# A four-layer convolution kernel: six-row sums in PSUM, border copies and a gate product on GpSimd, taps loaded a call ahead, box products behind the copies

## The chip, the cores and the metric

The kernel runs on one core of one Trainium2 chip. A core has five engines with in-order instruction queues of their own: TensorE (PE in the profile; PEld is its weight loads) for matrix products and transposes, VectorE (DVE) and ScalarE (ACT) for elementwise work, GpSimd (POOL), and SyncE (SP), which here only issues transfers. They work on two on-chip memories, SBUF and the smaller PSUM, which is cut into eight banks of 128 x 512 float32 values and into which TensorE writes; GpSimd has no part in PSUM anywhere in this kernel. Sixteen DMA engines move data to and from device memory; transfers are issued from the queues of SP, ACT and POOL. Engines wait for each other through semaphores. The metric is the device time of one execution in microseconds, and lower is better.

## The reference, cut to what matters

The input is x of shape (4, 384, 64, 64) in float32: four images, 384 channels. Four layers follow one another, and each adds its result to x: attention, a convolution with a Fourier filter in 8x8 patches, a token-mixing layer, and a 7x7 depthwise convolution whose filter depends on the image. The change concerns the end of the third layer and all of the fourth:

```python
# end of layer 2: h2 is a normalised hidden result, gate one number per image
ch = tok + h2
x = x + gate * ch + (1.0 - gate) * xn
# layer 3, on xn = group norm of x
x_w = gelu(x_avg @ w_avg.T + b_avg + x_max @ w_max.T + b_max)
xr = (x_w[:, :, None] * w_mix[None]).reshape(b, c, 7, 7)
Gx = sqrt(sum(xr * xr, axis=(2, 3)))
Nx = Gx / (mean over channels of Gx + 1e-6)
kern = gamma * (xr * Nx) + beta          # 7x7, one per image and channel
out = depthwise 7x7 convolution of xn with kern, zero padding 3
x = x + out
```

Since xr is one number per image and channel times a fixed 7x7 filter w_mix, the last convolution falls into two parts: a number times the convolution with w_mix, and beta times a 7x7 box sum. The kernel computes them apart and adds both to x.

## The kernel before, in words

Channels are in three tiles of 128 (NJ = 3, index j), each with four images (b) of 4096 pixels. Phases A, B and EF do the first three layers. Phase G (`phase_g`, L1686) is the last stage, and all that the change touches lies in it.

The code is written as Python generators that emit pieces of work in turn. A scheduler then orders the emitted instructions on each engine by their dependencies and its own estimates, so the order on an engine is close to, but not the same as, the order of the text. Tiles come from pools with a tag and a number of buffers: a tile's next use of a buffer waits for the last reader of its earlier use.

*The gate.* `x2_of(j, b)` (L1886) finishes x for one tile and image in four quarters of 1024 pixels: it loads a quarter of h2 (L1899, tag w7, three buffers), ScalarE multiplies and shifts it into a PSUM bank (L1903, two of 512), VectorE adds it to x (L1906), ScalarE sums squares (L1908) and VectorE takes the maximum (L1909). The finished x goes to device memory through GpSimd's queue (L1911). For tile 0, `to_strips` (L1914) at once makes the strips of the convolution from it: ScalarE scales (L1925), TensorE transposes (L1935), ScalarE and VectorE copy into the large SBUF tile z (L1942, L1940). For tiles 1 and 2 `half_strips` (L1848) does that later from device memory.

*The conv.* `conv7(j, c0)` (L1945) convolves eight channels with w_mix. Sixteen calls make one tile, 48 calls all three. A call loads its taps (L1950, 256 KB, through SP's queue, two buffers), makes four Toeplitz matrices from them and a band (L1959: two of three by VectorE with the band in PSUM, one of three by GpSimd with the band in SBUF), and multiplies them on TensorE with z (L1972) into a PSUM tile of 1024 columns (two banks, two buffers). For tiles 0 and 1 ScalarE copies the result out (L1981) and it goes to device memory (L1982); for tile 2 VectorE adds it to x from the box part (L1984), and the sum is output (L1985).

*The boxes.* `boxes(j, b)` (L1987) makes the 7x7 box sum of one tile and image in four parts of 16 rows. GpSimd adds pairs of rows (L2021) and neighbouring pairs (L2023); VectorE makes six-row sums in place (L2024) and adds to each the seventh row, which gives seven-row sums (L2029, L2030, L2034, with L2027 and L2038 at the image's border). Rows of the part before that a part needs are copied by ScalarE (L2003, L2016), and ScalarE fills border rows (L2008). TensorE transposes 4 x 128 columns at a time (L2044), ScalarE copies them to SBUF (L2046, tile ht), TensorE multiplies with a band matrix (L2050), which sums along the row, and VectorE scales and adds to x (L2052). For tiles 0 and 1 VectorE then adds the conv result, read back from device memory (L2062), and x is output (L2066); for tile 2 it goes to device memory (L2068) for `conv7` to add to.

*The order.* `phase_g` first runs the gate and the strips of tile 0, then for each tile the sixteen conv calls. After each call it takes pieces of other generators: with tile 0 the gate of tiles 1 and 2, with tiles 1 and 2 the boxes (first those of tile 2, then tile 0, then tile 1), and half strips of the tile that comes next. The boxes give up control three times a part, at these lines of the loop:

```python
            yield                       # L2039, after the seven-row sums
            for q in range(2):
                ...
                if q == 0:
                    yield               # L2053, after the first half
            ...
            yield                       # L2069, after the part
```

PSUM in this phase: three banks with tag m (`pm`), one for the band, four for the conv (two tiles of two banks).

## Time and profile before

| what | value |
|---|---|
| median of 3 runs | 4842.55 us (4839.95 to 4853.89) |
| the profiled execution's own time | 4841.52 us |
| its span in the profile | 4839.6 us, 49747 instructions |
| busy in the span: PE, DVE, ACT, POOL | 91%, 60%, 41%, 16% |
| phase G in the span | about 4070 to 4839.6 us |
| mean granted TensorE clock | 0.95 |

The busy shares are those of the whole span, in which the earlier phases weigh most: there TensorE alone is full. Phase G is read by stretches of its own. In it the first tile's gate ends at about 4163 us, the other gates at about 4362 us, and the rest is conv and boxes. A line of the profile names the line of the kernel, the engine, the operation, what it writes and reads and in what shape; a mean that is far above the median says that some of these instructions stood waiting after they had begun. In the chain of waits, "A <- B: total, times, longest" says how long A's engine sat idle until B was done.

### The profile page before, as it was taken

The page shows a single profiled execution, that of the slowest core. Times are in us where ns is not written, and L with a number is a line of the kernel's source. Part 1 is how long each engine was busy: PE and PEld are TensorE (multiplying, and loading weights), DVE is VectorE, ACT ScalarE, POOL GpSimd, SP SyncE. Part 2 cuts the span into 40 slices and gives each one's busy share as a digit, 9 for nine tenths or more (in the row PEclk, how much of TensorE's full clock was granted, in tenths as well). Part 3 has the DMA queues.
Part 4 walks back from the last instruction along what each step waited for, and adds up shares of the span by engine and source line. Part 5 has one row for each costly group of instructions (what it writes and reads, how often), then busy time and mean ns, then how long its engine had stood idle before and what let it go on. Part 6 is the DMA issues. An engine that isn't in the chain of part 4 may idle for free.

```text
span 4839.6 us, 49747 instructions
## 1 busy us (share of the span) xinstructions
PE 4399.5 (91%) x18445; PEld 2453.7 (51%) x18445; DVE 2892.0 (60%) x4647; ACT 1996.9 (41%) x2976; POOL 757.7 (16%) x643
## 2 busy tenths in 40 slices
PE   6999999999999999989987898699999997778888
PEld 2233444344443444435477787344444443678888
DVE  7766556645656455556867777555521113767898
ACT  4444444444444444336345566211133334763321
POOL 1000000000000000000044554000000001235544
PEclk9999999999999999989988999899999998788999
DMA  4312212111211111113168898776664444995776
GB/s 145 102 42 66 72 53 75 64 56 42 70 61 63 40 59 59 53 63 120 65 197 282 278 308 299 273 259 251 238 236 153 156 156 152 325 346 183 231 256 232
DMA packets 289663, 747.65 MB, mean 154 GB/s; under 512 B 22555, under 2 KB 123014, under 8 KB 277382
## 3 DMA queue, kind: packets, MB, share of 16 engines
q1 hardware_dynamic: 226744, 454.62, 29.4%
q0 software_dynamic: 36480, 167.01, 9.2%
q10 hardware_dynamic: 26190, 122.76, 6.4%
q8 instruction: 149, 2.44, 0.2%
q14 instruction: 100, 0.82, 0.1%
HBM read 442.04 MB, written 302.25 MB: 154 GB/s over the span
## 4 chain that ended last, share of the span: by engine, by line
PE 32%; DVE 7%; DMA 6%; ACT 3%; issue 2%; POOL 1%; SPq 0%; ACTq 0%; DVEq 0%; POOLq 0%
PE h_m L1658 10%; PE h_s L1604 10%; PE conv_m L1370 6%; PE conv_m L1972 2%; DMA c_d<-d 2%; DMA wmix<-in_mix_t 1%; DMA g_h<-h 1%; DVE toep L1959 1%; PE box_m L2050 1%; DVE in_x L2052 1%; DMA ax<-x 1%; DVE in_x L2062 1%; DMA unit_x<-x 1%; DVE box L2034 0%; ACT g_h L1908 0%
## 5 line engine op out<-in xcount | busy, mean ns | idle before, releaser
L819 ACT ACTIVATE probs<-sc_s 128x1024 f32<-128x1024 f32 x512 | 496.5, 1019 | 695.0 <-PE av L929 594.8
L929 PE MATMUL av<-probs,vt 128*128 128x512 f32 x1536 | 717.7, 604 | 0.0
L1128 DVE SCALAR_TENSOR_TENSOR acc<-band,vecs,acc 128x512 f32<-128x512 f32 x708 | 496.0, 745 | 44.9 <-POOL band L1089 39.6
L1658 PE MATMUL h_m<-f_h,cm_w_t 128*128 128x512 f32 x1152 | 497.3, 595 | 7.4 <-ACT f_h L1646 7.4
L1370 PE MATMUL conv_m<-toep,z 128*128 128x192 f32 (+1 forms) x2304 | 444.2, 354 | 9.5 <-DVE z L1299 9.4
L929 PEld LDWEIGHTS av<-probs,vt 128*128 128x128 f32 x1536 | 277.6, 192 | 339.6 <-issue 335.9
L1972 PE MATMUL conv_m<-toep,z 128*128 128x128 f32 x3072 | 395.5, 287 | 36.5 <-POOL toep L1959 15.8
L1370 PEld LDWEIGHTS conv_m<-toep,z 128*128 128x128 f32 x2304 | 408.5, 197 | 31.6 <-DVE z L1299 10.1
L1972 PEld LDWEIGHTS conv_m<-toep,z 128*128 128x128 f32 x3072 | 381.1, 203 | 38.4 <-POOL toep L1959 16.2
L1604 PE MATMUL h_s<-e_tok,cm_w_t 128*128 128x512 f32 x768 | 362.9, 595 | 4.2 <-DVE e_tok L1589 4.2
L1658 PEld LDWEIGHTS h_m<-f_h,cm_w_t 128*128 128x128 f32 x1152 | 220.4, 191 | 284.4 <-issue 273.3
L1666 DVE BATCH_NORM_STATS2 h_st<-f_h 128x6 f32<-128x512 f32 x96 | 66.5, 694 | 429.8 <-ACT f_h L1665 429.8
L811 PE MATMUL sc_s<-q,k 32*128 32x512 f32 x2048 | 307.1, 643 | 15.1 <-ACT probs L819 14.9
L1351 POOL TENSOR_TENSOR toep<-w,band 128x1280 f32<-128x1280 f32 x94 | 272.6, 2900 | 237.5 <-PE conv_m L1370 234.3
L1051 PE MATMUL t_m<-w_in_t,xb 128*128 128x384 f32 x768 | 282.0, 503 | 3.4 <-DVE coef L1068 3.2
L965 PE MATMUL proj_m<-xm,w_proj_t 128*128 128x512 f32 x576 | 270.3, 609 | 6.4 <-DVE xm L904 4.9
L1611 ACT COPY e_h<-h_s 128x1024 f32<-128x1024 f32 x96 | 97.2, 1012 | 400.2 <-PE h_s L1604 400.2
L1613 DVE BATCH_NORM_STATS2 h_st<-e_h 128x6 f32<-128x512 f32 x192 | 123.4, 685 | 204.9 <-ACT e_h L1611 204.7
L1604 PEld LDWEIGHTS h_s<-e_tok,cm_w_t 128*128 128x128 f32 x768 | 146.9, 191 | 187.9 <-issue 183.1
L1051 PEld LDWEIGHTS t_m<-w_in_t,xb 128*128 128x128 f32 x768 | 144.4, 194 | 141.6 <-issue 62.5
L972 DVE SCALAR_TENSOR_TENSOR x_res<-proj_m,bn_c,x_res 128x512 f32<-128x512 f32 x96 | 71.7, 747 | 240.2 <-PE proj_m L965 240.2
L1604 PE MATMUL h_s<-z,cm_w_t 128*128 128x512 f32 x384 | 196.7, 594 | 0.0
(423 smaller groups left out, 6396.3 us busy)
## 6 DMA issues: line engine op xcount, KB each, us to landing
d<-d_o ACTq DMA_DIRECT2D x48, 1024.0 KB
c_d<-d SPq DMA_DIRECT2D x48, 1024.0 KB
hid<-e_h ACTq DMA_DIRECT2D x16, 3072.0 KB
f_h<-hid SPq DMA_DIRECT2D x16, 3072.0 KB
x_in<-in_x SPq DMA_DIRECT2D x96, 256.0 KB
x_res<-in_x SPq DMA_DIRECT2D x32, 768.0 KB
xa<-x_res POOLq DMA_DIRECT2D x32, 768.0 KB, 3.9
xa_out<-xa SPq DMA_DIRECT2D x32, 768.0 KB
```

The costliest lines, as they stand in the source:

```text
L811: nc.tensor.matmul(s[:, g], lhsT=k4[32 * g : 32 * g + 32, c], rhs=q[i][32 * g : 32 * g + 32], start=True, stop=True,)
L819: nc.scalar.activation(p[:, h * 1024 : (h + 1) * 1024], s[:, 2 * h : 2 * h + 2].rearrange("p a b -> p (a b)"), AF.Exp, scale=0.25,)
L929: nc.tensor.matmul(av[0], lhsT=vt[:, 4 * c + v, :], rhs=p[:, v * 512 : (v + 1) * 512], start=c == 0 and v == 0, stop=c == 7 and v == 3,)
L965: nc.tensor.matmul(m, lhsT=self.w_proj[:, j, o * P : (o + 1) * P], rhs=xm[:, j], start=j == 0, stop=j == NJ - 1,)
L1051: nc.tensor.matmul(m[:, 0:C], lhsT=xb[:, j], rhs=self.w_in[:, j, :], start=j == 0, stop=j == NJ - 1,)
L1128: nc.vector.scalar_tensor_tensor(out, src(j, k), w, done, ALU.mult, ALU.add)
L1351: eng.tensor_tensor(t, self.w53[:, at : at + 160].rearrange("p (m n) -> p m n", n=8).unsqueeze(2).to_broadcast([P, 20, 8, 8]), band.rearra ...
L1370: nc.tensor.matmul(m[:, c * 256 + to : c * 256 + to + 64 * (k1 - k0)], lhsT=self.z_[:, at : at + P], rhs=t[:, 10 * c + k0 : 10 * c + k1].r ...
L1604: nc.tensor.matmul(s[:, v, :], lhsT=w1[:, j, o * P : (o + 1) * P], rhs=t[j][:, v * 512 : (v + 1) * 512], start=j == 0, stop=j == NJ - 1,)
L1613: nc.vector.bn_stats(st[:, o, 8 * b + 2 * i + v, :], h[:, o, v * 512 : (v + 1) * 512])
L1658: nc.tensor.matmul(m, lhsT=w2[:, o, j * P : (j + 1) * P], rhs=h[:, o, v * 512 : (v + 1) * 512], start=o == 0, stop=o == 5,)
L1972: nc.tensor.matmul(m[:, ch * P : (ch + 1) * P], lhsT=self.z_[:, at : at + P], rhs=t[:, 8 * c + 2 * i : 8 * c + 2 * i + 2].rearrange("p m a ...
```

## The change

The change has six parts, all in phase G.

- *Taps.* `load_mix` loads the taps of a call and keeps the tile in `mix_ahead`. It is called once before the loop, and each `conv7` takes that tile and calls it for the next call. The load is issued through GpSimd's queue instead of SP's.
- *conv7 as a generator.* `conv7` gives up control after each of its four matrices and at its end, and the loop takes the pieces of other generators there, five a call as before. Its PSUM tile is one bank of 512 columns, three buffers, and is copied out (or added) after every second matrix, in two halves instead of one.
- *Gate product of tile 0.* For j = 0, GpSimd multiplies and shifts h2 in place in SBUF, and VectorE adds 1024 columns at once from SBUF. Every second quarter takes its buffer from the pool with the tag rest, so that six are in use instead of three. For tiles 1 and 2 nothing changes.
- *Border rows.* The two row copies in `boxes` move from ScalarE to GpSimd. The fill reads a constant instead of x.
- *Six-row sums.* VectorE writes the six-row sum to a PSUM bank of its own (tag t) instead of back to SBUF, and the lines after it read it there. PSUM: three banks m, one band, three conv, one t.
- *Box products.* The product with the band matrix and the scaled addition move into `box_sums`, which is called after a yield that follows the ht copy, for both halves; the yield at the end of a part is gone, so there are still three.

```diff
@@ -1751,13 +1751,14 @@
             x2 = others(*(self.x2_of(j, b) for j in (1, 2) for b in range(B)))
             boxes = others(*(self.boxes(j, b) for j, b in ((2, 0), (2, 1), (2, 2), (2, 3), (0, 0), (0, 1), (0, 2), (0, 3))))
             boxes1 = others(*(self.boxes(1, b) for b in range(B)))
+            self.load_mix(0)
             for j in range(NJ):
                 for half in range(2):
                     strips = self.half_strips(j + half, 1 - half) if 0 < j + half < NJ else iter(())
                     for n in range(8):
-                        self.conv7(j, 64 * half + 8 * n)
-                        next(strips, None)
-                        for k in range(5):
+                        for k, _ in enumerate(self.conv7(j, 64 * half + 8 * n)):
+                            if k == 0:
+                                next(strips, None)
                             if j == 0 and (k < 2 or k == 2 and n % 2):
                                 next(x2, None)
                             if j == 1 or j == 2 and (k or n % 2):
@@ -1895,15 +1896,20 @@
         for q in range(4):
             sl = slice(q * 1024, (q + 1) * 1024)
 
-            h = self.gw_p.tile([P, 1024], F32, tag="w7", name="g_h2", bufs=3)
+            pool, tag = (self.gt_p, "rest") if j == 0 and q % 2 else (self.gw_p, "w7")
+            h = pool.tile([P, 1024], F32, tag=tag, name="g_h2", bufs=3)
             nc.sync.dma_start(h, self.h2[b][:, j, sl])
-            for v in range(2):
-                m = self.pm("x2_m")
-                part = slice(q * 1024 + v * 512, q * 1024 + v * 512 + 512)
-                nc.scalar.activation(
-                    m, h[:, v * 512 : v * 512 + 512], AF.Identity, bias=at(self.g0), scale=at(self.gh)
-                )
-                nc.vector.tensor_add(x[:, part], x[:, part], m)
+            if j == 0:
+                nc.gpsimd.tensor_scalar(h, h, at(self.gh), at(self.g0), ALU.mult, ALU.add)
+                nc.vector.tensor_add(x[:, sl], x[:, sl], h)
+            else:
+                for v in range(2):
+                    m = self.pm("x2_m")
+                    part = slice(q * 1024 + v * 512, q * 1024 + v * 512 + 512)
+                    nc.scalar.activation(
+                        m, h[:, v * 512 : v * 512 + 512], AF.Identity, bias=at(self.g0), scale=at(self.gh)
+                    )
+                    nc.vector.tensor_add(x[:, part], x[:, part], m)
 
             nc.scalar.activation(h, x[:, sl], AF.Square, bias=at(self.neg2), accum_out=self.x2_var[:, j, b, q : q + 1])
             nc.vector.tensor_reduce(self.x2_max[:, j, b, q : q + 1], x[:, sl], AX.X, ALU.max)
@@ -1942,17 +1948,26 @@
                     nc.scalar.copy(zv, mv.rearrange("p k c -> p c k"))
             yield
 
+    def load_mix(self, n):
+        if n < 16 * NJ:
+            c0 = n % 16 * 8
+            self.mix_ahead = self.gt_p.tile([P, 8 * 64], F32, tag="wmix", name="wmix")
+            src = self.ins["mix_t"][n // 16][:, c0 : c0 + 8]
+            self.nc.gpsimd.dma_start(self.mix_ahead, src.rearrange("p c t n -> p (c t n)"))
+
     def conv7(self, j, c0):
 
 
         nc = self.nc
-        wmix = self.gt_p.tile([P, 8 * 64], F32, tag="wmix", name="wmix")
-        nc.sync.dma_start(wmix, self.ins["mix_t"][j][:, c0 : c0 + 8].rearrange("p c t n -> p (c t n)"))
+        wmix = self.mix_ahead
+        self.load_mix(16 * j + c0 // 8 + 1)
         o = self.gt_p.tile([P, 8, P], F32, tag="rest", name="rest_o", bufs=3)
         if j == NJ - 1:
             nc.sync.dma_start(o, self.rest[c0 : c0 + 8].rearrange("c y b n -> (y b) c n"))
-        m = self.psum.tile([P, 1024], F32, tag="c", name="conv_m", bufs=2)
+        of = o.rearrange("p c n -> p (c n)")
         for pair in range(4):
+            if pair % 2 == 0:
+                m = self.psum.tile([P, 512], F32, tag="c", name="conv_m", bufs=3)
             t = self.gt_p.tile([P, 16, 8, 8], F32, tag="toep", name="toep", bufs=4)
             on_pool = (c0 // 2 + pair) % 3 == 2
             eng, band = (nc.gpsimd, self.band7) if on_pool else (nc.vector, self.band7_p)
@@ -1970,19 +1985,24 @@
                 for i in range(4):
                     at = (c0 + ch) * 136 + 4 * i
                     nc.tensor.matmul(
-                        m[:, ch * P : (ch + 1) * P],
+                        m[:, ch % 4 * P : (ch % 4 + 1) * P],
                         lhsT=self.z_[:, at : at + P],
                         rhs=t[:, 8 * c + 2 * i : 8 * c + 2 * i + 2].rearrange("p m a n -> p (m a n)"),
                         start=i == 0,
                         stop=i == 3,
                     )
-        of = o.rearrange("p c n -> p (c n)")
+            if pair % 2:
+                part = of[:, pair * 256 - 256 : pair * 256 + 256]
+                if j < NJ - 1:
+                    nc.scalar.copy(part, m)
+                else:
+                    nc.vector.tensor_add(part, part, m)
+            yield
         if j < NJ - 1:
-            nc.scalar.copy(of, m)
             nc.scalar.dma_start(self.raw[j][:, c0 : c0 + 8], o)
-            return
-        nc.vector.tensor_add(of, of, m)
-        nc.sync.dma_start(self.out[j][:, c0 : c0 + 8], o)
+        else:
+            nc.sync.dma_start(self.out[j][:, c0 : c0 + 8], o)
+        yield
 
     def boxes(self, j, b):
 
@@ -1991,7 +2011,6 @@
         nc = self.nc
         x = self.load_x2(j, b)
         off = lambda k: self.off[:, j, b, k - 6 : k - 5]
-        scale = self.b_s[:, j, b : b + 1]
         pairs_of = lambda t, r, n: t[:, r * W : (r + 2 * n) * W].rearrange("p (k r w) -> p k r w", r=2, w=W)
         above, last = None, None
         for part in range(4):
@@ -2000,20 +2019,20 @@
             if part < 3:
 
                 above = self.sm([P, 2, W], "edge")
-                nc.scalar.copy(above, pairs_of(x, r0 + 12, 2)[:, :, 1])
+                nc.gpsimd.tensor_copy(above, pairs_of(x, r0 + 12, 2)[:, :, 1])
 
             s = self.gw_p.tile([P, 10, W], F32, tag="w", name="box_2")
             t = self.gw_p.tile([P, 8, W], F32, tag="w6", name="box_6")
             h = self.gw_p.tile([P, 16 * W], F32, tag="w7", name="box_7", bufs=3)
             fill = lambda i: nc.scalar.activation(
-                s[:, i], x[:, r0 * W : (r0 + 1) * W], AF.Identity, bias=self.off[:, j, b, 2:3], scale=0.0
+                s[:, i], self.ident[:, 0:W], AF.Identity, bias=self.off[:, j, b, 2:3], scale=0.0
             )
             lo, hi = 2, 10
             if part == 0:
                 fill(0)
                 lo = 1
             else:
-                nc.scalar.copy(s[:, 0:2], last[:, 8:10])
+                nc.gpsimd.tensor_copy(s[:, 0:2], last[:, 8:10])
             if part == 3:
                 fill(9)
                 hi = 9
@@ -2021,7 +2040,9 @@
             nc.gpsimd.tensor_add(s[:, lo:hi], xv[:, :, 0], xv[:, :, 1])
             last = s
             nc.gpsimd.tensor_add(t, s[:, 0:8], s[:, 1:9])
-            nc.vector.tensor_add(t, t, s[:, 2:10])
+            six = self.psum.tile([P, 512], F32, tag="t", name="box_t", bufs=1).rearrange("p (k w) -> p k w", w=W)
+            nc.vector.tensor_add(six, t, s[:, 2:10])
+            t = six
             hv = pairs_of(h, 0, 8)
             if part == 0:
                 nc.vector.tensor_scalar(hv[:, 0:2, 0], t[:, 0:2], off(6), None, ALU.add)
@@ -2044,14 +2065,11 @@
                     nc.tensor.transpose(m[:, k * P : (k + 1) * P], h[:, at : at + P], self.ident)
                 ht = self.gt_p.tile([P, 512], F32, tag="ht", name="ht")
                 nc.scalar.copy(ht, m)
-                m = self.pm("box_m")
-                for k in range(4):
-                    sl = slice(k * P, (k + 1) * P)
-                    nc.tensor.matmul(m[:, sl], lhsT=ht[:, sl], rhs=self.cols7, start=True, stop=True)
-                xq = x[:, (2 * part + q) * 512 : (2 * part + q + 1) * 512]
-                nc.vector.scalar_tensor_tensor(xq, m, scale, xq, ALU.mult, ALU.add)
                 if q == 0:
                     yield
+                    self.box_sums(j, b, x, 2 * part, ht)
+            yield
+            self.box_sums(j, b, x, 2 * part + 1, ht)
             if j < NJ - 1:
                 d = self.gt_p.tile([P, 1024], F32, tag="rest", name="in_raw", bufs=3)
                 nc.sync.dma_start(
@@ -2066,7 +2084,16 @@
                     nc.gpsimd.dma_start(self.out[j].rearrange("(b m) c n -> b (m c n)", b=B)[b].rearrange("(c n) -> c n", c=P), x)
                 else:
                     nc.gpsimd.dma_start(self.rest[:, :, b], x.rearrange("p (y n) -> p y n", n=P))
-            yield
+
+    def box_sums(self, j, b, x, n, ht):
+
+        nc = self.nc
+        m = self.pm("box_m")
+        for k in range(4):
+            sl = slice(k * P, (k + 1) * P)
+            nc.tensor.matmul(m[:, sl], lhsT=ht[:, sl], rhs=self.cols7, start=True, stop=True)
+        xq = x[:, n * 512 : (n + 1) * 512]
+        nc.vector.scalar_tensor_tensor(xq, m, self.b_s[:, j, b : b + 1], xq, ALU.mult, ALU.add)
 
 
 @with_exitstack
```

## The prediction

> **What bounds the kernel now.** Everything that the change touches runs after 4070 us, so I first cut the last stage into four stretches (busy time by engine, then granted clock, DMA share, GB/s): the gate of the first channel tile, the conv of that tile with the other gates, and two halves of conv and boxes.
>
> ```profile
> core 0: us, PE busy (x) PEld busy (x) DVE busy (x) ACT busy (x) POOL busy (x), PEclk, DMA share, GB/s
> 4077.00:4163.00 86.00, 34.35 (x132) 22.85 (x132) 58.08 (x76) 80.64 (x105) 9.14 (x19) 0.52 0.87 310
> 4163.00:4362.00 199.00, 156.25 (x1228) 153.72 (x1228) 136.28 (x157) 118.59 (x171) 64.24 (x39) 0.88 0.95 340
> 4362.00:4610.00 248.00, 214.70 (x1735) 208.14 (x1736) 207.55 (x249) 89.76 (x162) 134.94 (x99) 0.94 0.68 206
> 4610.00:4840.00 230.00, 193.60 (x1573) 188.48 (x1571) 208.53 (x210) 45.60 (x94) 105.13 (x64) 0.93 0.73 241
> ```
>
> Stretch 1 is ScalarE's (80.6 of 86), with DMA close behind. Stretch 2 is the DMA engines': share 0.95, in most of it 0.97 to 0.99. Stretches 3 and 4 have two near-bounds at once, TensorE and VectorE; in stretch 4 VectorE leads (it has nothing to do after 4828).
>
> Second, VectorE's own lines (min/median/max ns), to see whether 208 us is work or waiting:
>
> ```profile
> L2024 DVE TENSOR_TENSOR box<-box,box x48: 660/690/2882, 4367.2 to 4803.2; 128x512 f32<-128x512 f32 x48
> L2029 DVE SCALAR_TENSOR_TENSOR box<-edge,off,box x36: 317/344/4112, 4374.9 to 4804.9; 128x128 f32<-128x128 f32 x36
> L2052 DVE SCALAR_TENSOR_TENSOR in_x<-box_m,b_s,in_x x96: 727/740/752, 4377.4 to 4827.9; 128x512 f32<-128x512 f32 x96
> L2062 DVE SCALAR_TENSOR_TENSOR in_x<-in_raw,a_s,in_x x32: 1271/1276/3419, 4533.2 to 4828.6; 128x1024 f32<-128x1024 f32 x32
> ```
>
> The lines with two SBUF inputs (L2024, L2029, L2062) reach four to twelve times their minimum; L2052, with one input in PSUM, never varies. The timeline shows why:
>
> ```profile
> 4698.57 2.69 POOL L1959 TENSOR_TENSOR toep<-wmix,band 128x1024 f32<-128x1024 f32 x1 [2.91 <-PE conv_m L1972]
> 4698.96 1.21 DVE L1959 TENSOR_TENSOR toep<-wmix,band_p 128x1024 f32<-128x1024 f32 x1
> ...
> 4700.09 1.72 DVE L2034 SCALAR_TENSOR_TENSOR box<-in_x,off,box 128x512 f32<-128x512 f32 x1
> ```
>
> L2034 (median 740 ns) begins while GpSimd multiplies and ends at 4701.81, some 0.55 us after GpSimd's end at 4701.26. The VectorE product before it, with its band in PSUM, ran at full speed under the same GpSimd instruction. So part of VectorE's busy time is a lock.
>
> Third, the chain of waits:
>
> ```profile
> ACT box L2016 <- DVE box L2024: 81.6, 23, 9.7
> POOL toep L1959 <- DMA wmix<-in_mix_t: 62.6, 8, 16.6
> ACT edge L2003 <- DVE box L2029: 55.0, 26, 7.2
> PE box_m L2050 <- ACT ht L2046: 38.4, 23, 5.4
> ```
>
> TensorE waits 38 us for the ht copies, which stand on ScalarE behind border copies that wait for VectorE. The taps' waits are all but a little in stretch 2, where bandwidth rules anyway.
>
> **What the skill says.** The Trainium skill, SBUF — State Buffer, section "SBUF: two separate sides": VectorE and GpSimd share one port pair as an exclusive lock held for a whole instruction, taken by a VectorE op with two SBUF inputs against a GpSimd op that reads SBUF; the loser blocks. The lines above agree (344 ns against up to 4112). VectorE: DVE Perf Modes, "Why PSUM operands drop a tier": a PSUM operand keeps a float32 op at 1x; L2052 at 740 ns equals L2034's median of 740 from SBUF, so a PSUM input costs nothing seen here. GPSIMD Engine Reference, section 4.1, for a price: two-input ops about twice VectorE's time, one-input roughly line rate; the trace has 2.36 us against 1.21 us for the two-input product.
>
> **The change part by part.**
>
> *Six-row sums in PSUM.* L2024 still reads two SBUF tensors and keeps its stalls; its readers L2029, L2030, L2034, L2027, L2038 now have at most one SBUF input. Their excess (mean of the stretch less median, times count): stretch 3: (934-344) x 21 + (717-607) x 29 + (896-740) x 21 + (1178-607) x 7 + (897-368) x 8 ns = 12.4 + 3.2 + 3.3 + 4.0 + 4.2 = 27.1 us. Stretch 4: (870-344) x 15 + (1008-607) x 19 + (1157-740) x 15 + (610-274) x 5 = 7.9 + 7.6 + 6.3 + 1.7 = 23.5 us. Remaining excess: L2024 9.7 and 9.2, L2062 0.9 and 10.4. These can grow: a GpSimd that is less often blocked, and busier, meets them more. Bounds for the whole edit on VectorE: 50.6 us gained, or, if all goes to L2024 and L2062, nothing. I take all of it minus 2 us for 24 single-input ops of 128 columns that may lose a fast mode.
>
> *Border copies to GpSimd.* 72 copies leave ScalarE (36 x 298 + 36 x 297 ns = 21 us, and 55 + 82 us of queue-blocking waits). On GpSimd no 128-column copy is seen; 128x192 copies took 387 to 423 ns (L1089, L1090), so about 0.35 us each, bounds 0.15 (a memset) to 0.6 (L1103): 15 us in stretch 3, 9 in stretch 4. Behind a waiting copy on GpSimd stand the next pair sums, one product in three, and the tap loads; see the third rival.
>
> *Taps a call ahead on GpSimd's queue.* 48 loads leave SP (0.34 us issue each) and cost GpSimd about 0.585 us each (the similar loads of L1337): 9.4 us per stretch of 16. Each waits only for products a call back. Freed: 81 us of waits, but in stretch 2 under saturated DMA.
>
> GpSimd then has 134.9 + 15 + 9.4 = 159 us of 248 and 105.1 + 9 + 9.4 = 124 of 230: not a bound by volume.
>
> *Box products behind the copies.* After the change conv matmuls, usually eight, stand between the transposes and their box products, where before it was often four. Of 21.3 + 17.1 us of waits I let a quarter stay.
>
> *Two half-evacuations.* ScalarE 32 x 1.00 becomes 64 x 0.58: +5 us, hidden (89.8 us busy in 248). VectorE 16 x 1.209 becomes 32 x 0.683 (L1906's shape): +2.5 us in stretch 4.
>
> *Gate product of tile 0 on GpSimd.* ScalarE loses 32 x 0.774 = 24.8 us of 80.6. VectorE has 16 adds of 1024 (about 1.22) in place of 32 of 512 at 0.683: -2.3 us, and up to 16 x 2 = 32 us of lock. GpSimd gains 16 products; none such is in the trace. Bounds: 1.0 us at line rate, 2.36 as the two-input product, 4.8 if L1103's 597 ns for 128 columns is all slope. I take 2.0: 32 us. ScalarE's 56 us plus about 10 of start and strip tail, or VectorE's 58 + 10 of lock, end stretch 1 at some 68 to 72 us: about 15 earlier by the engines. DMA decides what of it lasts: busy 0.87 x 86 + 0.95 x 199 = 264 us for the same bytes; at 0.97 that is 272 instead of 285, 13 at best. I take 10.
>
> **Sum.** Stretches 1 and 2: -10. Stretch 3: TensorE is the longer engine at 214.7, with 33.3 idle; three quarters of 21.3 gone leaves 17.3, so 232: -16. Stretch 4: VectorE 208.5 - 23.5 - 0 + 2.5 + 1 = 188.5 falls below TensorE's 193.6, which cannot shrink (40 conv matmuls take 4.47 us back to back even at the end); with about 16 us idle, 209: -21. Total -47. The profiled execution took 4841.5 (span 4839.6), so 4794.5; the runs' median is 4842.55, one higher: **4795**.
>
> **Rivals.** *Half the gain:* the lock moves to L2024 and L2062 and throttling (clock 0.93 to 0.94) eats TensorE's denser work. For it: L2062 already reaches 3.4 us; against: over half of the locked time is in lines now immune. Gain 23: 4820. *Nothing shows:* TensorE's idle time is kept by the strip loads (27 us of ACT waits for them) and every gain stays off the path; the stage-1 gain is given back to DMA. 4840; against it, VectorE at 40 of 40 us between 4760 and 4800 (39.96 busy). *Slower, by GpSimd's queue:* in stretches 3 and 4 GpSimd already waits 110 us for VectorE (27.7 + 13.1 + 17.0 and 29.8 + 15.5 + 6.9). The moved copies bring 55 + 82 = 137 us of the same kind. Room in my 441 us: 441 - 159 - 124 - 110 = 48. From 48 us added on, it eats the gain; from 85 on it ends slower; in full, 283 + 110 + 137 = 530 against 478, +52 - 10: 4884. For it: one queue, in order; against: the copies wait for much the same VectorE progress as the pair sums behind them, and the early release of the four-row sums (now by L2024's successor alone) takes away most of 57.5 + 28.5 us. *GpSimd product at 4.8 us:* stretch 1 would be 77 + 5 for the pair scales, no gain there: 4805, inside the range.
>
> **How the numbers follow.** Likeliest, 4775 to 4815: 0.55. More than that, with TensorE's idle time nearly gone (about 4765): 0.10. Half: 0.15. Nothing, within 0.3% (14.5 us, about what can be told from no change): 0.08. Slower: 0.12. The range 4765 to 4836 leaves out the slower case, part of the no-change case and half of the better one.
>
> **What will show it.** L2030 and L2034's successors with maxima near 0.75 us; L2024's and L2062's means not above 1.2 and 1.9 us; TensorE's wait for ht under 12 us; the product on GpSimd at 1 to 2.4 us and the first tile's gate done by 4150; GpSimd's waits in stretches 3 and 4 under 160 us. The prediction is wrong if TensorE or VectorE waits for box sums or taps from GpSimd for tens of us, or if the middle 0.95 DMA share only turns into more waiting.

## The result and the profile after

The changed kernel takes 4780.78 us (median of four runs, 4770.85 to 4787.78) against 4841.25 us for the kernel before, measured beside it: a ratio of 0.9875, 95% interval 0.9858 to 0.9891, or 60 us less. Measured a second time, beside other runs of the kernel before, it took 4792.5 us, ratio 0.9895 (0.9879 to 0.9911), 50 us less. The forecast was 47 us less.

Part of that spread lies outside the change. In the fourteen profiles of this study the last matrix product ahead of phase G starts between 4059.9 and 4078.3 us, though the work up to there is the same. So I read the profiles by the length of phase G, from that product to the end: 770.7 us before, 715.1 and 721.3 in the two profiles of the changed kernel. It is cut where the work says so: at the first conv product, at the first product of the factors, at the last ScalarE evacuation of conv sums, and at the end. Before (busy time by engine, then granted clock, DMA share, GB/s):

```profile
core 0: us, PE busy (x) PEld busy (x) DVE busy (x) ACT busy (x) POOL busy (x), PEclk, DMA share, GB/s
4068.90:4163.50 94.60, 35.50 (x137) 23.39 (x135) 63.50 (x109) 82.22 (x109) 11.38 (x24) 0.54 0.82 292
4163.50:4360.50 197.00, 154.72 (x1215) 152.19 (x1215) 135.72 (x156) 117.31 (x170) 64.24 (x39) 0.88 0.96 342
4360.50:4602.90 242.40, 209.13 (x1688) 202.79 (x1689) 200.86 (x243) 88.89 (x161) 133.60 (x97) 0.94 0.67 201
4602.90:4839.60 236.70, 200.66 (x1633) 195.32 (x1631) 215.31 (x219) 47.24 (x97) 106.47 (x65) 0.94 0.74 246
```

After:

```profile
core 0: us, PE busy (x) PEld busy (x) DVE busy (x) ACT busy (x) POOL busy (x), PEclk, DMA share, GB/s
4064.00:4143.60 79.60, 32.45 (x136) 26.73 (x134) 62.31 (x91) 61.10 (x77) 38.07 (x43) 0.52 0.90 331
4143.60:4336.20 192.60, 150.88 (x1139) 147.92 (x1140) 139.08 (x161) 119.48 (x184) 74.89 (x60) 0.85 0.99 352
4336.20:4571.60 235.40, 212.35 (x1776) 208.56 (x1775) 182.35 (x243) 81.72 (x133) 154.71 (x152) 0.94 0.69 218
4571.60:4779.10 207.50, 188.11 (x1621) 185.79 (x1619) 185.81 (x230) 40.61 (x70) 122.59 (x107) 0.97 0.83 272
```

Stretch by stretch that is -15.0, -4.4, -7.0 and -29.2 us (-14.7, -3.0, -4.8 and -26.9 in the second profile). The fourth gained most, and there VectorE is down by 30 us and TensorE by 13. The second is now full: DMA share 0.99.

The border between stretches 2 and 3 moved with respect to the work: before, 1146 conv products fell into stretch 2 and 910 into stretch 3, after it 1071 and 979 (the box products of stretch 3 are 400 and 415). At 0.13 us for a conv product (395.5 us for 3072, before), that is some 10 us of work, an estimate, that stretch 2 handed to stretch 3. So these two are best read together: -11.4 us, and -7.8 in the second profile.

VectorE's own lines after (min/median/max ns): the six-row sum (L2044, L2024 before), the three seven-row sums, and the addition of the conv result (L2080, L2062 before):

```profile
L2044 DVE TENSOR_TENSOR box_t<-box,box x48: 680/700/2664, 4319.2 to 4752.6; 128x512 f32<-128x512 f32 x48
L2050 DVE SCALAR_TENSOR_TENSOR box<-edge,off,box_t x36: 326/336/347, 4336.2 to 4755.3; 128x128 f32<-128x128 f32 x36
L2051 DVE SCALAR_TENSOR_TENSOR box<-in_x,off,box_t x48: 568/603/609, 4322.7 to 4755.6; 128x384 f32<-128x384 f32 x48
L2055 DVE SCALAR_TENSOR_TENSOR box<-in_x,off,box_t x48: 584/732/744, 4324.4 to 4756.8; 128x512 f32<-128x512 f32 x36, 128x384 f32<-128x384 f32 x12
L2080 DVE SCALAR_TENSOR_TENSOR in_x<-in_raw,a_s,in_x x32: 1268/1286/3287, 4497.9 to 4766.7; 128x1024 f32<-128x1024 f32 x32
```

The three lines with one input in PSUM no longer vary (L2029, now L2050, reached 4112 ns). The two that still have both inputs in SBUF do.

The chain of waits after, phase G alone:

```profile
ACT box L2027 <- DVE box_t L2044: 52.0, 16, 9.0
ACT ax L1865 <- DMA ax<-x: 48.7, 14, 8.7
POOL wmix L1956 <- DVE toep L1974: 28.5, 16, 3.2
POOL wmix L1956 <- issue: 26.9, 7, 10.4
PE box_m L2094 <- ACT ht L2067: 21.2, 9, 5.0
```

Border fills on ScalarE still wait for VectorE, and more than before (11.7 us then, when the copies did most of the waiting). TensorE waits 21 us for the ht copies where it waited 38. New is the second line's size (27.3 us before), and the third and fourth are new waits: GpSimd stands idle ahead of the tap loads that the change gave it.

### The profile page after: what moved, and what is told of

It is laid out like the page before. It is cut to its first block, busy times and chain, and to the rows that moved or that the text cites. A ratio compares the mean times of both kernels' runs of the same rounds, so it can differ in the third digit from the quotient of the medians.

```text
span 4779.1 us, 49753 instructions
## 1 busy us (share of the span) xinstructions
PE 4377.5 (92%) x18445; PEld 2442.5 (51%) x18445; DVE 2846.8 (60%) x4647; ACT 1964.3 (41%) x2904; POOL 832.4 (17%) x779
## 5 line engine op out<-in xcount | busy, mean ns | idle before, releaser
L811 PE MATMUL sc_s<-q,k 32*128 32x512 f32 x2048 | 306.6, 642 | 14.9 <-ACT probs L819 14.7
L1351 POOL TENSOR_TENSOR toep<-w,band 128x1280 f32<-128x1280 f32 x94 | 272.3, 2897 | 240.0 <-PE conv_m L1370 236.8
L1611 ACT COPY e_h<-h_s 128x1024 f32<-128x1024 f32 x96 | 97.2, 1013 | 399.6 <-PE h_s L1604 395.5
L1604 PE MATMUL h_s<-z,cm_w_t 128*128 128x512 f32 x384 | 196.1, 592 | 0.0
```

Of the source, the lines that this page charges most:

```text
L811: nc.tensor.matmul(s[:, g], lhsT=k4[32 * g : 32 * g + 32, c], rhs=q[i][32 * g : 32 * g + 32], start=True, stop=True,)
L1351: eng.tensor_tensor(t, self.w53[:, at : at + 160].rearrange("p (m n) -> p m n", n=8).unsqueeze(2).to_broadcast([P, 20, 8, 8]), band.rearra ...
L1604: nc.tensor.matmul(s[:, v, :], lhsT=w1[:, j, o * P : (o + 1) * P], rhs=t[j][:, v * 512 : (v + 1) * 512], start=j == 0, stop=j == NJ - 1,)
```

## The experiments

Each kernel is compared with runs of the kernel before, made beside it. The table has the ratio with its interval, and from one profiled execution the length of phase G and its stretches in us. The two profiles of the changed kernel differ by 6 us in phase G, so less than that says nothing.

| kernel | ratio (95%) | phase G | stretches 1 to 4 |
|---|---|---|---|
| before | 1 | 770.7 | 94.6, 197.0, 242.4, 236.7 |
| changed | 0.9875 (0.9858 to 0.9891) | 715.1 | 79.6, 192.6, 235.4, 207.5 |
| changed again (e12) | 0.9895 (0.9879 to 0.9911) | 721.3 | 79.9, 194.0, 237.6, 209.8 |
| six in SBUF, in place (e1) | 0.9959 (0.9944 to 0.9973) | 749.4 | 80.7, 190.7, 247.1, 230.9 |
| six in SBUF, own buffer (e7) | 0.9951 (0.9936 to 0.9966) | 742.4 | 80.5, 192.8, 242.8, 226.3 |
| before + six in PSUM (e6) | 0.9964 (0.9945 to 0.9983) | 755.9 | 94.5, 204.7, 236.8, 219.9 |
| borders on ScalarE (e2) | 0.9904 (0.9887 to 0.9920) | 728.6 | 79.7, 193.8, 238.5, 216.6 |
| box products direct (e3) | 0.9893 (0.9878 to 0.9909) | 718.7 | 79.7, 189.1, 235.5, 214.4 |
| gate on ScalarE (e4) | 0.9913 (0.9899 to 0.9926) | 726.6 | 96.2, 190.4, 234.6, 205.4 |
| taps in the call, SyncE (e5) | 0.9863 (0.9845 to 0.9880) | 700.9 | 77.7, 184.1, 233.1, 206.0 |
| steps after whole calls (e8) | 0.9902 (0.9885 to 0.9918) | 718.0 | 80.5, 192.7, 226.5, 218.3 |
| strips in five pieces (e9) | 0.9893 (0.9875 to 0.9911) | 719.6 | 83.6, 189.0, 235.8, 211.2 |
| taps ahead, SyncE (e10) | 0.9857 (0.9838 to 0.9876) | 701.6 | 79.8, 193.6, 224.6, 203.6 |
| no strip loads (e11) | 0.9785 (0.9771 to 0.9799) | 670.1 | 79.5, 170.0, 216.8, 203.8 |

**Two theories.** *Lock:* the gain is VectorE's time, which its operations with two SBUF inputs lost to GpSimd's. *Queue:* it is in the moved copies and box products, so that ScalarE and TensorE no longer stand behind one another. The first experiments undo one part each.

**e1, the six-row sums back in SBUF.**

```diff
-            six = self.psum.tile([P, 512], F32, tag="t", name="box_t", bufs=1).rearrange("p (k w) -> p k w", w=W)
-            nc.vector.tensor_add(six, t, s[:, 2:10])
-            t = six
+            nc.vector.tensor_add(t, t, s[:, 2:10])
```

> The changed kernel with the six-row sums back in SBUF, in place; everything else stays. Lock theory (VectorE's two-SBUF-input operations wait for GpSimd): the seven-row sums have maxima above 2 us again where they now end at 0.35 to 0.75, VectorE's busy time in the last two stretches grows by 20 to 50 us, and of the 36 us that these stretches gained 15 to 30 are lost: 4796 to 4811. Queue theory (the gain is in the copies and box products that no longer hold up ScalarE and TensorE; VectorE had slack): VectorE is busier all the same, but the time stays at 4781, give or take 7.

Measured 4823.82 us: 31 to 43 us are lost, more than the lock theory said, and in phase G 28 to 34. VectorE is busy 210.3 us in stretch 4, 24.5 more. Where this reaches TensorE is in e1's chain of waits, where the first two rows had 0.7 and 4.0 us after the change:

```profile
PE ht_m L2063 <- DVE in_x L2094: 15.2, 8, 4.5
PE strip_m L1869 <- DVE in_x L2094: 15.0, 8, 2.7
...
DVE box L2043 <- POOL box L2042: 25.6, 17, 3.5
```

L2094 is VectorE's scaled addition, which empties the PSUM bank that the next transposes need. That line itself is never slow (0.72 to 0.75 us); it comes late, behind seven-row sums that stand in the lock. The third row is a second effect: VectorE waits for GpSimd's four-row sums, which the changed kernel's chain doesn't have.

**e7, the same sums in an SBUF buffer of their own.** In e1 the four-row sum's buffer is also released later (after the seven-row sums), so GpSimd can start its next pair sums less early. e7 gives the six-row sum its own buffer.

```diff
-            t = self.gw_p.tile([P, 8, W], F32, tag="w6", name="box_6")
+            t = self.gw_p.tile([P, 8, W], F32, tag="w6", name="box_6", bufs=1)
...
-            six = self.psum.tile([P, 512], F32, tag="t", name="box_t", bufs=1).rearrange("p (k w) -> p k w", w=W)
+            six = self.gw_p.tile([P, 8, W], F32, tag="w6b", name="box_t", bufs=1)
```

> The changed kernel with the six-row sum in a buffer of its own in SBUF in place of the PSUM bank (one buffer for it, one for the four-row sum, so that the memory is the same). The four-row sum's buffer is then free as early as with PSUM, but the seven-row sums have two SBUF inputs. Lock theory: as with the sums in place, 4810 to 4830, with their maxima above 2 us. Release theory (the gain is that GpSimd's next pair sums start earlier): 4781 to 4790.

Measured 4815.26 us, phase G 742.4: 21 to 27 us lost. Its lines for the seven-row sums, and a new wait of GpSimd:

```profile
L2050 DVE SCALAR_TENSOR_TENSOR box<-edge,off,box_t x36: 332/374/3566, 4333.3 to 4770.0; 128x128 f32<-128x128 f32 x36
L2051 DVE SCALAR_TENSOR_TENSOR box<-in_x,off,box_t x48: 601/609/3321, 4318.2 to 4775.0; 128x384 f32<-128x384 f32 x48
L2055 DVE SCALAR_TENSOR_TENSOR box<-in_x,off,box_t x48: 585/751/2948, 4320.0 to 4776.1; 128x512 f32<-128x512 f32 x36, 128x384 f32<-128x384 f32 x12
...
POOL box L2042 <- DVE box_t L2044: 53.8, 30, 4.8
```

The instructions are the same, and the release is as early; besides the memory of one input only the four-row sum's second buffer is gone. GpSimd waits 54 us for the one that is left, but VectorE waits for none of GpSimd's box sums, as in the changed kernel, so the buffer isn't what costs the time. The maxima go from 0.35, 0.61 and 0.74 us to 3.6, 3.3 and 2.9. Of the 132 instructions of these lines 39 take over 1.3 times the shortest of their shape. All 39 overlap an elementwise instruction of GpSimd, and 38 of them end a fixed time after it ends: 0.15, 0.42 or 0.55 us for 128, 384 or 512 columns. In the changed kernel 85 of the 132 overlap one too, and none is slow. So it is the memory of that input, as the Trainium skill has it (SBUF — State Buffer, "SBUF: two separate sides"). As in e1, TensorE meets the lateness at L2096, the scaled addition: its waits there are 32 us (25.1 for strips, 7.1 for transposes), 4.7 in the changed kernel. The 7 us between e7 and e1 would be the earlier release, but is no more than two profiles differ by.

**e6, the kernel before with only the six-row sums in PSUM.** To make room, conv sums are in three banks with two evacuations a call, as in the changed kernel.

```diff
-        m = self.psum.tile([P, 1024], F32, tag="c", name="conv_m", bufs=2)
         for pair in range(4):
+            if pair % 2 == 0:
+                m = self.psum.tile([P, 512], F32, tag="c", name="conv_m", bufs=3)
...
-            nc.vector.tensor_add(t, t, s[:, 2:10])
+            six = self.psum.tile([P, 512], F32, tag="t", name="box_t", bufs=1).rearrange("p (k w) -> p k w", w=W)
+            nc.vector.tensor_add(six, t, s[:, 2:10])
+            t = six
```

> The kernel before with only the six-row sums moved to a PSUM bank (and, to make room for it, conv sums in three banks of 512 columns with two evacuations a call). Putting them back cost the changed kernel 43 us. If that is VectorE's lock and nothing else, the edit is worth the same alone: 4796 to 4812. If VectorE's lock only counts once ScalarE and TensorE no longer wait for one another (the moved copies, the box products a step later), it is worth little alone: 4825 to 4842.

Measured 4824.64 us, at the edge of the second case. Stretches 3 and 4 got 22.4 us shorter (undone in e1 they got 31 to 35 longer), with VectorE busy 173 and 192 us instead of 201 and 215; but stretch 2 took 204.7 us, 7.7 more, where TensorE waits 46 us for Toeplitz matrices in place of 31, for a reason that no run here shows. So about two thirds of what the edit is worth in the changed kernel comes without the other parts, and a third of that is lost again elsewhere. It also does much of what the border copies were moved for: with these still on ScalarE, its copies and fills wait 70 us for VectorE in place of 148, and TensorE's wait for ht copies is 26.9 us in place of 38.4.

**e2, the border copies back on ScalarE** (the two `nc.gpsimd.tensor_copy` of `boxes` as `nc.scalar.copy` again).

> The changed kernel with the 72 border copies back on ScalarE. Queue theory: ScalarE stands behind VectorE again (above 80 us of such waits in the last two stretches), TensorE's wait for the ht copies goes from 21 to 35 us or more, and 8 to 16 us are lost: 4789 to 4797. Lock theory: the copies were no part of the gain: 4781, give or take 7. GpSimd-queue theory (its in-order queue costs something, only less than it saves): GpSimd loses 21 us of copies and some 50 us of waits, box sums come earlier: 4765 to 4775.

Measured 4798.91 us; phase G is 7 to 13 us longer, 7 to 9 of them in stretch 4. ScalarE stands behind VectorE for 112 us in place of 52 in the last two stretches:

```profile
ACT box L2035 <- DVE box_t L2044: 66.7, 26, 7.1
...
ACT box L2027 <- DVE box_t L2044: 23.4, 10, 5.6
ACT edge L2022 <- DVE box L2050: 21.8, 18, 3.8
```

The place is as the queue theory had it, the mechanism not wholly: TensorE's box products wait 19.4 us for the ht copies, no more than after the change; what grew is its strip transposes' wait for those copies, from 5.0 to 12.4 us. By the medians the loss is 6 to 18 us, and the interval overlaps both of the changed kernel's. The third case, a faster kernel, did not come.

**e3, box products directly behind their copies.**

```diff
+                self.box_sums(j, b, x, 2 * part + q, ht)
                 if q == 0:
                     yield
-                    self.box_sums(j, b, x, 2 * part, ht)
-            yield
-            self.box_sums(j, b, x, 2 * part + 1, ht)
```

The yield returns to the end of the part.

> The changed kernel with each group of box matmuls issued right behind its ht copy, not a step later. If the distance to the copy is what cut TensorE's wait (38 to 21 us): the wait is back at 35 to 45 us and most of the difference shows, since TensorE is the longest engine: 4790 to 4800. If TensorE would only have waited elsewhere (taps' products, conv banks): the wait for ht grows, others shrink as much, 4781, give or take 7.

Measured 4790.89 us, between the two measurements of the changed kernel; phase G 718.7 us, the same. The wait for ht copies is 25.7 us, not 35 to 45. So the distance did little by itself.

**e4, the gate product of tile 0 back on ScalarE** (`x2_of` as before the change, so with three buffers for h2 again, not six).

> The changed kernel with the gate product of tile 0 back on ScalarE, in PSUM. The 19 us gained before the factors are this edit's: stretch 1 takes 93 to 95 us instead of 80 and stays lost: 4791 to 4798. If the DMA engines were the bound of the first two stretches together, the second is shorter by what the first is longer, 4781 to 4786. If the product on GpSimd had hurt (the lock against the adds, 16 products of 1.2 us), it would be faster: below 4775.

Measured 4796.66 us. Its first two stretches (columns as above):

```profile
4071.40:4167.60 96.20, 36.76 (x137) 24.41 (x135) 63.60 (x109) 82.51 (x110) 13.02 (x27) 0.52 0.81 289
4167.60:4358.00 190.40, 149.29 (x1140) 145.44 (x1141) 138.63 (x160) 118.35 (x183) 74.89 (x60) 0.89 0.99 349
```

Stretch 1 is 16.5 us longer, stretch 2 only 2 to 4 shorter. The gain of this part in both together, 13 to 14 us, stays; the DMA engines took back a fifth of it at most. Phase G as a whole is 5 to 12 us longer, and the interval overlaps that of e12: the part shows in its stretches, hardly in the total. What its product and what its three more buffers gained was not told apart.

**e8, the steps after each whole conv call.**

```diff
-                        for k, _ in enumerate(self.conv7(j, 64 * half + 8 * n)):
-                            if k == 0:
-                                next(strips, None)
+                        for _ in self.conv7(j, 64 * half + 8 * n):
+                            pass
+                        next(strips, None)
+                        for k in range(5):
```

> The changed kernel with the gate and box steps after each whole conv call, five in a row, as in the kernel before, not one after each channel pair. If the spread of the steps matters: TensorE finds its box work with VectorE and ScalarE still behind, waits for ht copies rise from 21 to above 40 us, and 10 to 25 us are lost, in the last two stretches: 4791 to 4806. If each engine's queue has enough ahead either way: 4781, give or take 7.

Measured 4791.12 us, phase G 718.0, the wait for ht 15.3 us. Stretch 3 is shorter and stretch 4 longer by about as much. No worth of the spread of the steps can be seen here.

**e5 and e10, the taps.** e5 loads them in the call again, on SyncE's queue; e10 keeps them a call ahead and changes the queue alone.

```diff
-            self.nc.gpsimd.dma_start(self.mix_ahead, src.rearrange("p c t n -> p (c t n)"))
+            self.nc.sync.dma_start(self.mix_ahead, src.rearrange("p c t n -> p (c t n)"))
```

> The changed kernel with each call's taps loaded inside that call again, on SyncE's queue. If the taps were on the path in the last two stretches: VectorE's and GpSimd's waits for taps, 17 and 34 us now, pass 80 us and the stage is 8 to 15 us longer: 4789 to 4796. If their waits lay in the second stretch only, where the DMA engines are full (share 0.99), or beside TensorE's other work: 4781, give or take 7. If GpSimd's queue was short of time, it gains 28 us there and the kernel is faster: below 4774.

> The changed kernel with the taps still a call ahead, but issued on SyncE's queue. Loading them inside the call on SyncE gave 4773, 8 us less than the changed kernel, nearly all of it in the second stretch. If GpSimd's queue was the harm (24 us of waits at the issue there, products behind it): 4766 to 4775, and with the earlier issue not slower than inside the call. If issuing ahead was the harm (the load's buffer is the one that the call before still reads, so the issue waits, and on SyncE the gate's and strips' loads would wait behind it): 4781 to 4795.

Measured 4772.8 and 4770.58 us, phase G 700.9 and 701.6: both are faster than the changed kernel, by 14 to 20 us of phase G. (Where it shows, stretch 2 or 3, depends on how much conv work was done by the factors; the sum of both is 428.0 and 431.6 after the change, 417.2 and 418.2 here.) In stretch 2 of the changed kernel:

```profile
POOL wmix L1956 <- issue: 23.7, 5, 10.4
PE conv_m L1987 <- DVE toep L1974: 20.6, 8, 5.4
...
PE conv_m L1987 <- POOL toep L1974: 10.6, 2, 6.5
```

and of e10:

```profile
PE conv_m L1987 <- DVE toep L1974: 8.6, 2, 4.6
...
PE conv_m L1987 <- POOL toep L1974: 7.3, 2, 6.3
```

TensorE waits 31.2 us for Toeplitz matrices against 15.9. The waits ahead of the loads are called "issue", which means that the profile names nobody who ended them. The longest:

```profile
4178.99 0.58 POOL L1956 DMA_DIRECT2D wmix<-in_mix_t  x1 [10.38 <-issue]
```

The trace does show what it waited for. This is the load for call 5, and the taps have two buffers, so it fills the one that call 3 read. VectorE's last Toeplitz product of call 3 starts at 4177.23 and ends at 4178.44 us; the load starts 0.55 us later. It is the same with six of the seven waits of this kind (26.6 of 26.9 us): each ends 0.54 to 0.56 us after VectorE's last product of the call two before the load's. The 28.5 us in the chain of waits, which the profile does put down to VectorE's products, are the same kind of wait. So a load issued a call ahead waits for its buffer, and on GpSimd's queue the pair sums and products stand behind that wait, 55 us in all. In e10 the loads wait for their buffers too, up to 15.7 us, but on SyncE's queue, where none of GpSimd's work stands behind them. Issuing earlier gained nothing (e5 is as fast as e10); together with GpSimd's queue it did harm. A third buffer was not tried. The Trainium skill (SBUF — State Buffer, "SBUF: two separate sides") says that GpSimd writes the descriptors of transfers from its queue itself and can be locked out by VectorE, and advises the queues of ScalarE or SyncE; the runs agree with the advice, but the long waits here are for the buffer.

**e9 and e11, the strip loads.** Stretch 3 became 7 us shorter where 16 were said. e9 cuts the strips into five pieces with three buffers, spread over the calls:

```diff
+PIECES = ((0, 7), (7, 7), (14, 7), (21, 6), (27, 6))
...
-            for part in range(3):
-                y = self.gt_p.tile([P, 11 * P], F32, tag="y", name="ax2", bufs=2)
+            for part, (k1, nk) in enumerate(PIECES):
+                y = self.gt_p.tile([P, 7 * P], F32, tag="y", name="ax2", bufs=3)
...
-                            if k == 0:
+                            if (5 * n + k) % 3 == 0:
                                 next(strips, None)
```

> The changed kernel with the strips of the conv's input cut into five pieces of 7, 7, 7, 6 and 6 x 128 columns with three buffers, in place of three of 11 with two, and one piece every three steps; the bytes are the same. Stretch 3 gained 7 us where 16 were said; ScalarE stands 49 us behind strip loads (14 times, up to 8.7 us) that start only when a buffer is free, and the ht copies stand behind it. If that is what held stretch 3: these waits fall below 20 us, TensorE's wait for ht from 21 to under 12 us, and stretch 3 takes 222 to 229 us in place of 235: 4766 to 4776. If the loads only give way to another wait (GpSimd's pair sums, rest and in_x2 loads on SyncE's queue): 4781, give or take 7. The smaller transfers and four more z copies for each half could cost up to 6 us: not above 4790.

Measured 4790.33 us: no gain, and no test of the theory, since the waits did not go away. In e9:

```profile
ACT ax L1868 <- DMA ax<-x: 70.0, 21, 8.8
PE box_m L2097 <- ACT ht L2070: 35.1, 11, 6.3
```

Both grew. Yet phase G took 719.6 us, as in the changed kernel, with 14 us more of waits for ht: such a wait isn't by itself time lost. (The strips of tile 0 are cut in the same way, and stretch 1 took 4 us more.) e11 therefore leaves the loads out:

```diff
-                for u in range(2):
-                    src = self.scratch["x2"][2 * pair + u][j][64 * half : 64 * half + 64]
-                    nc.sync.dma_start(y[64 * u : 64 * u + 64, inside], src[:, max(lo, 0) : min(hi, N)])
...
-                nc.scalar.activation(y[:, inside], y[:, inside], AF.Identity, bias=b, scale=s)
+                rows = (min(hi, N) - max(lo, 0)) // W
+                nc.scalar.activation(
+                    y[:, inside].rearrange("p (r w) -> p r w", w=W),
+                    self.ident[:, 0:W].unsqueeze(1).to_broadcast([P, rows, W]),
+                    AF.Identity, bias=b, scale=s,
+                )
```

> The changed kernel without the strip loads of tiles 1 and 2 from device memory (some 34 MB of transfers): ScalarE scales a constant tile into the strip instead, so that the conv of tiles 1 and 2 is of other data, and all else stays. It bounds what the strip loads hold. If ScalarE's 49 us behind these loads, with the ht copies queued behind it, are why stretch 3 gained 7 us and not 16: stretch 3 takes 220 to 227 us in place of 235, and the second stretch, where the loads share full DMA engines, gets 10 to 20 us shorter too: 4745 to 4765. If stretch 3 is held by TensorE and VectorE whatever the loads do, only the second stretch gets shorter: stretch 3 at 231 or more, 4760 to 4775.

(The 34 MB there is a slip; two tiles of four images are 2 x 4 x 128 x 4096 x 4 bytes = 16.8 MB, and a little overlap.) Measured 4740.56 us, below the range:

```profile
4150.90:4320.90 170.00, 141.01 (x1123) 138.58 (x1123) 136.47 (x163) 116.67 (x182) 73.61 (x61) 0.90 0.94 362
4320.90:4537.70 216.80, 210.43 (x1792) 206.56 (x1793) 181.30 (x240) 82.43 (x135) 158.10 (x151) 0.97 0.59 200
```

```profile
PE box_m L2096 <- ACT ht L2069: 7.2, 5, 2.5
```

Stretch 3 takes 217 us instead of 235 to 238, of which TensorE is busy 210, and the wait for ht copies in it falls from 14.6 to 0.9 us (7.2 in phase G). The changed kernel's own trace tells the same. In stretch 3 its chain of work that ended last has, for example (start us, us, what; pieces under 1.2 us are left out):

```profile
4485.55 9.76 DMA ax<-x
4495.44 1.43 issue
4497.49 2.08 PE box_m L2094 x8
```

A strip load lands, ScalarE scales the strip (1.56 us from 4495.40) and only then makes the ht copy that stood behind it in its queue (from 4496.87), and the box products follow at 4497.49. Followed back one by one, 13.5 of the 14.6 us of stretch 3 end behind a strip that waited for its load; the rest, and all 6.5 us of stretch 4, end behind a border fill that waited for VectorE. So in stretch 3 the wait for ht is ScalarE's wait for strip loads, handed on. e11 takes more away than that: 16.8 MB from the DMA engines and the loads from SyncE's queue. It bounds what the loads cost in every way, and its largest gain, 23 us, is in stretch 2, which has no ht copies.

**e12, the changed kernel again.**

> The changed kernel once more, beside the same runs of the kernel before, to set the spread: a ratio of 0.986 to 0.989, and 76 to 80, 190 to 195, 232 to 238 and 205 to 211 us in the four stretches. If the profile of the first run was a lucky one, the last two are longer, by up to 10 us together.

Measured 4792.5 us, just above the expected ratios; each stretch is inside its range, and the last two are together 4.5 us longer. With it, e3, e8 and e9 can't be told from the changed kernel, and by the whole time e2 and e4 hardly.

## Why the prediction was right, and where not

The time, 4795 us for the likeliest case, was right to 14 us in the first measurement and 3 in the second. That the sum came out so near is partly luck: stretches 1 and 2 together and stretch 4 gained more than said, stretch 3 less, and the taps took 14 to 20 us that the forecast had at nothing. With them on SyncE's queue (e10) phase G is 69 us shorter than before, against the 47 of the forecast. By its steps:

*The lock.* Right, and the main cause. The seven-row sums have no excess left. The means of L2044 are 1156 and 1046 ns, of L2080 1683 and 1652, under the 1.2 and 1.9 us named; the excess of both together is 12.3 + 3.6 = 16 us in stretch 3 and 6.6 + 8.4 = 15 in stretch 4, where 9.7 + 0.9 and 9.2 + 10.4 were there before. So in stretch 3, with more box work in it than before, it grew by 5 us, and in stretch 4 it shrank by as much: the lock did not move to these two lines.

*Stretch 4, -21.* It was -29.2 and -26.9. The mis-sized term is "TensorE's 193.6, which cannot shrink". At the boundaries used here TensorE went from 200.7 us for 1633 products to 188.1 for 1621, while the granted clock went from 0.94 to 0.97; with the sums in SBUF again (e1) it was 196.1 at 0.94. The clock's rise would be some 6 of these 13 us (an estimate: 200.7 x 0.94 / 0.97 = 194.5), the 12 products fewer 1 or 2; the rest is open. VectorE's 185.8 us and the 16 us of idle time, measured 19, were as estimated.

*Stretch 3, -16.* It was -7.0 and -4.8. Of the 9 us short in the first profile 3 are TensorE's busy time, 212.4 us in place of 209.1, with the work that stretch 2 had handed on; the other 6 are its idle time, 33.3 us before, 23.1 after, 17.3 forecast. The step that failed is "three quarters of 21.3" us gone by putting conv products between copy and box product. The wait fell to 14.6 us only, and in the whole phase to 21.2 where under 12 was named. e3 shows that this part does almost nothing by itself. What went wrong is the reading of the wait: it was put down to border copies that wait for VectorE. Followed back in the trace before the change, that holds (with border fills) for 12.0 of the 21.3 us in stretch 3 and for all 17.1 in stretch 4, but 8.3 us in stretch 3 stood behind strip loads. After the change the first kind is down to 1.1 us, and the second is up to 13.5. The "nothing shows" rival had named just that ("TensorE's idle time is kept by the strip loads"), and for what is left in this one stretch it was right.

*Stretches 1 and 2, -10.* They were -19.4 and -17.7, of which stretch 1 is 15. Right that ScalarE's 24.8 us come off stretch 1 (-15 said, -15.0 measured) and that the product is no slower than 2 us: it took 1.205 (median), and the first gate was done by 4143.6 us. Wrong was how much the DMA engines take back: the share in both stretches together was 0.97, which is the bound named, but against 0.91 before over the whole 291.6 us (the forecast left out the first 8), which leaves room for 17, not 13, and I took less still. e4 gives 2 to 4 us taken back of 16.5. Stretch 2 itself gained little or nothing: its 4.4 us are the conv work handed on, TensorE's idle time in it is 42.3 us before and 41.7 after, and its DMA share went from 0.96 to 0.99. The sign of being wrong that named this share came near for stretch 2 alone.

*Taps, costed at nothing.* This failed. The freed waits were hidden, as said, and the 48 loads were small "by volume". But "each waits only for products a call back" is true and was left without a price: with GpSimd's queue behind it, that wait is 55 us, and 14 to 20 us of phase G (e5, e10). The forecast looked for harm from GpSimd's queue at the border copies; it came from the loads.

*Slower, by GpSimd's queue.* Fell. Its waits for VectorE in the last two stretches, 135 us in all before, of which the forecast counted 110, went down to 96 (25.3 + 24.0 + 18.5 + 15.8 + 7.2 and some small ones), not up by 137: the six-row sum releases the four-row sum's buffer at once, and the copies wait in place of the pair sums, much as the argument against this rival had it. A copy takes 0.29 us, 0.35 was said. Two slips there: the 85 us from which "it ends slower" leave out the 10 us gained in stretches 1 and 2, with which it is 95; and VectorE's last instruction before the change starts at 4834.1, not by 4828 us.

What is not accounted for: undone one by one, the parts cost about 31 (six-row sums), 10 (borders), 8 (gate), 0 (products, steps) and give 17 (taps), against the mean of the two profiles: 32 together of some 52 in phase G. The rest is in no single part that was undone. The conv's three smaller banks and the fill's constant were never undone alone, and e6 shows that parts depend on each other.

A version that is faster than the kernel before, and by phase G than the changed one, is the changed one with its taps on SyncE's queue, a call ahead (e10): 4770.58 us, 0.9857 of the kernel before. Its interval overlaps the changed kernel's first and not its second; phase G is shorter than in either profile.

## What to carry to other kernels

When a line's maximum is several times its minimum in a view by source line, ask which of its inputs could be in another memory: here one PSUM bank for one operand was worth some 31 us of phase G, the moved copies 10 and the moved product 8. A wait that ends at a copy is not the copy's own: follow what stands ahead of it in its engine's queue before you pay for distance behind it. And cost a transfer on an engine's queue by how long it waits for its buffer and by what that engine does for others just behind it, not by the issue's length. When you compare stretches, count the work in them: a border that moves shows a gain in one and a loss in the other.

## What the runs showed of the hardware that was not expected

- A multiply-and-add of 128x1024 with one SBUF input took GpSimd 1.205 us, no longer than VectorE's two-input addition of that size (1.221 us); twice that was feared. The Trainium skill's price (GPSIMD Engine Reference, section 4.1: about line rate for one input) fits.
- In the lock a VectorE operation of 128, 384 or 512 columns ended 0.15, 0.42 or 0.55 us after GpSimd's instruction, however long it had taken by then (38 of the 39 slow ones in e7).
- GpSimd stood 55 us ahead of the 48 tap loads, 27 of them for nothing that the profile names; in the trace nearly all of these waits end 0.3 to 0.56 us after a VectorE product that reads the load's buffer.
- The six-row sum is hardly slower for writing to PSUM (700 ns against 690 in SBUF), but keeps its stalls (up to 2.66 us): with both inputs in SBUF, an output in PSUM did not help it.
- Where stretch 4 has the same 1620 or 1621 products, TensorE's busy time goes with the granted clock: 196 us at 0.93 and 0.94 (e7, e1), 188 and 189 at 0.97 (the changed kernel, twice), 185 at 0.99 (e4, e10). What set the clock is not shown.
